# A graph layer's edge loop: VectorE and ScalarE in a written order, node-span products in halves, registers and keys for two chunks at a time

## The chip, the cores and the metric

One core of a Trainium2 chip. The metric is device time in microseconds (us); lower is better. Profile lines are of one profiled execution.

## The reference

12,500 nodes with 32 features, 400,000 edges sorted by their target node, 32 features per edge, a two-layer network on each edge, and a maximum over the edges of a node:

```python
h = jnp.maximum(_layernorm(x, axis=-1), 0.0)
e_feat = jnp.concatenate([h[src], h[dst], edge_attr_32], axis=-1)   # 400000 x 96
hid = jax.nn.relu(e_feat @ W1 + b1)                                 # 96 -> 64
v = hid @ W2 + b2                                                   # 64 -> 32
x_cand = jax.ops.segment_max(v, dst, num_segments=12500)
out = x + jnp.maximum(x_cand, h)
```

## The kernel before

The edges are cut into four stripes, which lie on the four quarters of the partitions. A chunk is 512 edges of each stripe; there are 196 chunks, and the main loop (L363) takes two chunks, a pair, per step. Ahead of it, the kernel computes h, writes it to memory (`h_d`), multiplies it by the target part of W1 (`q_d`) and writes both the keys of the edges whose rows are found by matmul (`key_d`) and the penalties between nodes (`pen_d`). After it, the maxima are merged and added.

One step of the loop does this for its two chunks:

- `gather` (L139): the source rows of h. 12 of a chunk's 16 groups of rows come by indirect DMAs from GpSimd into `gh`, six buffers of one chunk each, 24 DMAs per pair. A buffer is free when VectorE has transposed it (L324).
- `rows_by_matmul` (L278): the other four groups ("tiles") of each chunk, found by TensorE. VectorE makes one-hot matrices out of the keys `kb`: seven `hot` (L285) and one `its` (L287). For a tile, TensorE sums 15 matmuls in a `pv` buffer: one with `its` (L292) and 14 with `hot` (L295). VectorE's maximum (L297) picks the row into `gm`. The generator yields after each tile, and the loop asks for eight tiles per step, for the chunks of the next step.
- `load` (L301): edge features `ea` (SyncE), targets `db` and penalties `pb` (ScalarE's queue), four chunks at once. SyncE loads four registers for a chunk (L314) and fetches four windows of `q_d` by them, `qw` (L318).
- `into_ph` (L375): the first layer, summed in four `ph` buffers out of `ea`, out of `of` and `qw` (`of` is the one-hot matrix of the target, L370), and out of the transposed rows `ht`. `to_features` (L321) makes `ht` by transposes of `gh` (L324) and `gm` (L326).
- ScalarE's relu gives `hid` (L389); the second layer goes into two `pv` buffers (L399); VectorE's scan (L404) gives the running maximum `sm`.
- `leave_1` (L332): TensorE transposes `sm` (L336), VectorE adds b2 (`so`, L338) and makes `last`, which marks the last edge of each node (L340).
- `leave_2` (L346): four matmuls (L350) bring the marked rows to their places in the nodes' windows, ScalarE copies the result to `wo` (L353), and SyncE writes the four blocks on the diagonal to `top_d` by the same registers (L357).

The `pv` pool has three buffers, for tiles and the second layer alike; `tr`, of `leave_1` and `leave_2`, has one. What sets the order:

```python
            tc.manual_schedule(engines={SP, PE}):
```

SyncE and TensorE run as the program is written. On VectorE, ScalarE and GpSimd a scheduler chose the order when the kernel was built. For a pair, VectorE's instructions stand as: two transposes of `gh` for the pair after, two tile maxima, `so`, scan, `its`, scan, maximum, seven `hot`, maximum, a transpose of `gm`, `last`, maximum, `so`, maximum, `last`, `its`, maximum, one `hot`, a transpose of `gm`, six `hot`, two `of`, maximum. On TensorE: `ea`, `of`, tile, `ht`, two tiles, transposes, second layer, two tiles, products (the pair before's second chunk), tile, transposes, tile, products, tile.

Of the kernel before, what the change touches and what calls it, by code (L numbers as in the profile page):

```python
# [18 lines left out]
SP = mybir.EngineType.SP  # L19
PE = mybir.EngineType.PE  # L20
DVE = mybir.EngineType.DVE

P = 128
N = 12500
# [34 lines left out]
def gnn_kernel(ctx, tc, x, src, src_mm, src_t, dst, dst_next, dst_ext, lo, hi, edge_attr, weights, w1, w2, b2, out):  # L59

# [40 lines left out]
    lo_i = const.tile([1, NS, NCH], I32, name="lo_i")  # L101
    nc.sync.dma_start(lo_i, lo.rearrange("(o s) c -> o s c", o=1))

    ident = const.tile([P, P], F32, name="ident")
    make_identity(nc, ident)
# [33 lines left out]
    def gather(c):  # L139
        gh = gathered.tile([P, K, D], F32, name="gh")  # L140
        for k in range(K - MM * (c in MMC)):
            if c * C + k * D < SE:
                nc.gpsimd.indirect_dma_start(  # L143
                    out=gh[:, k, :], out_offset=None, in_=h_d[:, :],
                    in_offset=bass.IndirectOffsetOnAxis(ap=src_i[:, c, k:k + 1], axis=0))
        return gh
# [123 lines left out]

    ea_v = edge_attr.rearrange("s f e -> (s f) e")
    with tc.tile_pool(name="edges", bufs=3) as pool, tc.tile_pool(name="edges_ps", bufs=1, space=PSUM) as ps, \
            tc.manual_schedule(engines={SP, PE}):
        loaded = {}
        windows = {}
        mm_rows = {}

        def rows_by_matmul():  # L278

            for i, c in enumerate(MMC):  # L280
                kb = pool.tile([P, 2, MM * P], F16, name="kb", bufs=2)
                nc.scalar.dma_start(kb, ap(key_d, i * MM * P, [[0, P], [len(MMC) * MM * P, 2], [1, MM * P]]))
                hot = pool.tile([P, A1, MM * P], F32R, name="hot", bufs=2)
                for k in range(A1):
                    nc.vector.tensor_scalar(hot[:, k], kb[:, 0], key_p[:, k:k + 1], None, op0=ALU.is_equal)  # L285
                its = pool.tile([P, MM * P], BF16, name="its", bufs=2)
                nc.vector.tensor_scalar(its, kb[:, 1], place, None, op0=ALU.is_equal)  # L287
                gm = mm_rows[c] = pool.tile([P, MM, D], F32, name="gm", bufs=6)
                for m in range(MM):
                    e = slice(m * P, (m + 1) * P)  # L290
                    po = ps.tile([P, C], F32, name="pv", bufs=3)[:, :D * A0]
                    nc.tensor.matmul(po, its[:, e], others.rearrange("p f a -> p (f a)"), start=True, stop=False)  # L292
                    for k in range(A1):
                        for part in range(2):
                            nc.tensor.matmul(po, hot[:, k, e], hs[:, part, k].rearrange("p f a -> p (f a)"),  # L295
                                             start=False, stop=(k == A1 - 1 and part == 1))
                    nc.vector.tensor_reduce(gm[:, m, :], po.rearrange("p (f a) -> p f a", a=A0),  # L297
                                            axis=AX.X, op=ALU.max)
                    yield

        def load(c):  # L301
            if c % LOAD == 0:
                n = min(LOAD, NCH - c) * C
                ea = pool.tile([P, LOAD * C], F32, name="ea", bufs=2)
                nc.sync.dma_start(ea[:, :n], ea_v[:, c * C:c * C + n])
                db = pool.tile([P, LOAD * C], I32, name="db", bufs=2)
                pb = pool.tile([P, LOAD * C], BF16, name="pb", bufs=2)
                for s in range(NS):
                    g = slice(s * D, (s + 1) * D)
                    nc.scalar.dma_start(db[g, :n], ap(dst_ext, 1 + s * S + c * C, [[0, D], [1, n]]))  # L310
                    nc.scalar.dma_start(pb[g, :n], ap(pen_d, s * S + c * C, [[0, D], [1, n]]))
                for k in range(c, min(c + LOAD, NCH)):
                    loaded[k] = [t[:, (k - c) * C:(k - c + 1) * C] for t in (ea, db, pb)]
            _, base = nc.values_load_multi_w_load_instructions(  # L314
                lo_i[0:1, :, c], engines=[SP], min_val=0, max_val=N)
            qw = pool.tile([P, HID], F32, name="qw", bufs=6)
            for s in range(NS):
                nc.sync.dma_start(qw[s * W:(s + 1) * W, :], q_d[bass.ds(base[s], W), :])  # L318
            windows[c] = qw, base

        def to_features(c, gh):  # L321
            ht = pool.tile([P, K, D], F32, name="ht", bufs=4)
# [6 lines left out]
                nc.vector.memset(ht[:, n:], 0.0)  # L329
            return ht.rearrange("p k e -> p (k e)")  # L330

        def leave_1(c, sm):  # L332
# [6 lines left out]
            last = pool.tile([P, J, NS, W], F32, name="last", bufs=2)  # L339
            nc.vector.tensor_tensor(  # L340
                last, iota_w[:, None, None, :].to_broadcast([P, J, NS, W]),
                at[:, :, c * J:(c + 1) * J].rearrange("p s j -> p j s")[:, :, :, None].to_broadcast([P, J, NS, W]),
                op=ALU.is_equal)
            return so, last

        def leave_2(c, so, last):  # L346

            pw = ps.tile([P, J, P], F32, name="tr")[:, 0]
            for j in range(J):
                nc.tensor.matmul(pw, last[:, j].rearrange("p s w -> p (s w)"), so[:, j, :],  # L350
                                 start=(j == 0), stop=(j == J - 1))
            wo = pool.tile([P, P], F32, name="wo")
            nc.scalar.activation(wo, pw, AF.Copy)  # L353
            _, base = windows.pop(c)
            for s in range(NS):
                g = slice(s * W, (s + 1) * W)
                nc.sync.dma_start(top_d[s % 2][bass.ds(base[s], W), :], wo[g, s * D:(s + 1) * D])  # L357

        tiles = rows_by_matmul()
        for c in range(AHEAD):  # L360
            load(c)
        sm = None
        for c in range(0, NCH, 2):  # L363
            for k in range(c + AHEAD, min(c + AHEAD + 2, NCH)):
                load(k)
            gh = [gather(c + x) for x in range(2)]
            of = []
            for x in range(2):
                of.append(pool.tile([P, C], F32, name="of", bufs=4))
                nc.vector.tensor_scalar(of[x], loaded[c + x][1], node[:, c + x:c + x + 1], None, op0=ALU.is_equal)  # L370


            ph = [ps.tile([P, C], F32, name=f"ph{s}") for s in range(NS)]
# [1 line left out]
            def into_ph(pairs, start, stop):  # L375
                for s in range(NS):
                    g = slice(s * D, (s + 1) * D)
                    for x, (w, e) in enumerate(pairs):
                        nc.tensor.matmul(ph[s][x * HID:(x + 1) * HID], w[g], e[g], start=start, stop=stop)  # L379

            into_ph([(w1c, loaded[c + x][0]) for x in range(2)], True, False)
            into_ph([(windows[c + x][0], of[x]) for x in range(2)], False, False)
            next(tiles, None)
            ht = [to_features(c + x, gh[x]) for x in range(2)]
            into_ph([(w1a, ht[x]) for x in range(2)], False, True)
            hid = []
            for s in range(NS):
                hid.append(pool.tile([P, C], F32, name="hid", bufs=6))
                nc.scalar.activation(hid[s], ph[s], AF.Relu, bias=b1c)  # L389
            next(tiles, None)  # L390
            next(tiles, None)

            if c > 0:
                left = leave_1(c - 1, sm)
            pv = [ps.tile([P, C], F32, name="pv", bufs=3) for x in range(2)]
            for s in range(NS):
                for x in range(2):
# [2 lines left out]
            sms = []  # L400
            for x in range(2):
                before = -LOW if sm is None else sm[:, C - 1:C]
                sm = pool.tile([P, C], F32, name="sm", bufs=4)
                nc.vector.tensor_tensor_scan(sm, loaded.pop(c + x)[2], pv[x], before, op0=ALU.add, op1=ALU.max)  # L404
# [12 lines left out]

    with tc.tile_pool(name="out", bufs=1) as pool:
# [152 lines left out]
```

## Time and profile before

| | |
|---|---|
| median of 3 runs | 5232.83 us (5221.43 to 5245.07) |
| profiled execution | 5227.3 us, span 5225.5 us |
| mean granted clock of TensorE | 0.81 |
| TensorE matmul / weight load busy | 3638.2 us (70%) / 2775.9 us (53%) |
| VectorE busy | 1846.3 us (35%) |
| GpSimd busy | 2238.9 us (43%) |
| ScalarE busy | 315.6 us (6%) |

In the profile, PE is TensorE's matmuls and PEld its weight loads, DVE is VectorE, ACT ScalarE, POOL GpSimd, SP SyncE; a q behind the name means the engine's instruction queue, which issues DMAs and waits. A line of a group reads: line, engine, operation, written tile <- read tiles, shapes, count, then busy us and mean ns of one, then the engine's idle time just before these instructions and what ended it. "issue" is time in which the engine waited for nothing that the profile shows; "remote" is a release that the profile can't put down to an instruction. In the timeline, a line has start and duration in us, and in brackets the idle time before it. Matmul starts are those of the hand-over by TensorE's sequencer, and their ends are modelled. "Records" are single matmuls of the trace: a float32 matmul gives two, all others one.

### The profile page before, as it was taken

Reading aid. Unit: us, or ns where it says so; the run is one execution under the profiler, and the core shown is the slowest. Engines: PE = TensorE matmul, PEld = TensorE weight load, DVE = VectorE, ACT = ScalarE, POOL = GpSimd, SP = SyncE. Lnnn points to the kernel's source line nnn. Section 1 sums busy time; section 2 is a strip of 40 time slices with the busy share of each in tenths; the row PEclk is TensorE's granted clock in tenths of the full one; section 3 lists DMA queues with packets and bytes.
Section 4 is the critical chain, followed back from the end, with each engine's and each line's share of the span. In section 5 each row is a group of like instructions: output and inputs, shape, how many; then the busy total and the mean of one; then the engine's idle time right before and its main releaser. Section 6 shows DMA issues by size and latency. Waiting matters only on the chain. (4 is left out here: it accounts for less than half of the span.)

```text
span 5225.5 us, 57318 instructions
## 1 busy us (share of the span) xinstructions
PE 3638.2 (70%) x20281; PEld 2775.9 (53%) x20281; DVE 1846.3 (35%) x3612; ACT 315.6 (6%) x627; POOL 2238.9 (43%) x2369
## 2 busy tenths in 40 slices
PE   2376767676767676767676767676767676777687
PEld 1255555555555555555554555555555555555565
DVE  2333333333333333333333333333333333333344
ACT  1000000000000000000000000000000000000000
POOL 6534344444444444444444444444444444444420
PEclk6587878787878787878788888787878787878788
DMA  3321112211211121112111211121112211211121
GB/s 123 90 58 43 42 39 58 44 41 40 58 42 41 40 56 44 40 40 56 44 40 40 57 44 40 40 56 44 41 40 57 44 41 40 57 44 40 40 53 65
DMA packets 235577, 256.47 MB, mean 49 GB/s; under 512 B 123653, under 2 KB 211861, under 8 KB 222102
## 3 DMA queue, kind: packets, MB, share of 16 engines
q10 hardware_dynamic: 74084, 137.60, 9.7%
q0 software_dynamic: 75296, 38.70, 5.6%
q1 hardware_dynamic: 85906, 76.48, 4.9%
q8 instruction: 159, 2.61, 0.2%
q14 instruction: 132, 1.08, 0.1%
HBM read 238.44 MB, written 14.04 MB: 48 GB/s over the span
## 5 line engine op out<-in xcount | busy, mean ns | idle before, releaser
L143 POOL DMA_INDIRECT gh<-h_d,src_i x2353 | 2234.8, 950 | 2812.1 <-DVE ht L324 2098.3
L295 PE MATMUL pv<-hs,hot 128*128 128x448 f32 x10808 | 2874.0, 413 | 712.6 <-issue 712.4
L295 PEld LDWEIGHTS pv<-hs,hot 128*128 128x128 f32 x10808 | 2282.8, 212 | 1444.9 <-issue 1270.9
L297 DVE TENSOR_REDUCE gm<-pv 128x32 f32<-128x448 f32 x772 | 481.2, 623 | 2548.3 <-remote 1529.4
L292 PE MATMUL pv<-others,its 128*128 128x448 bf16 x772 | 301.9, 391 | 427.0 <-issue 386.0
L285 DVE TENSOR_SCALAR hot<-kb,key_p 128x512 fp32r<-128x512 f16 x1351 | 555.8, 479 | 9.5 <-DMA qw<-q_d 9.5
L350 PE MATMUL tr<-so,last 128*128 128x128 f32 x1568 | 250.2, 282 | 250.0 <-issue 240.8
L404 DVE TENSOR_TENSOR_SCAN sm<-pb,sm,pv 128x512 f32<-128x512 bf16 x195 | 248.9, 1276 | 469.3 <-remote 332.5
L350 PEld LDWEIGHTS tr<-so,last 128*128 128x128 f32 x1568 | 227.1, 197 | 229.5 <-issue 211.8
L389 ACT ACTIVATE hid<-ph,wt 128x512 f32<-128x512 f32 x392 | 239.3, 690 | 973.5 <-PE ph L379 529.9
L292 PEld LDWEIGHTS <-its 128*128 128x128 bf16 x772 | 78.0, 101 | 400.5 <-issue 387.4
L353 ACT ACTIVATE wo<-tr 128x128 f32<-128x128 f32 x196 | 54.5, 278 | 3810.7 <-remote 1817.6
L336 PE MATMUL tr<-ident,sm 128*128 128x128 f32 x784 | 146.0, 319 | 22.3 <-ACT wo L353 22.3
L336 PEld LDWEIGHTS tr<-ident,sm 128*128 128x128 f32 x784 | 117.9, 167 | 57.9 <-ACT wo L353 38.4
L338 DVE TENSOR_TENSOR so<-tr,wt 128x512 f32<-128x512 f32 x196 | 133.9, 683 | 24.1 <-PE pv L292 11.5
L340 DVE TENSOR_TENSOR last<-iota_w,at 128x512 f32<-128x512 f32 x196 | 131.6, 672 | 28.2 <-PE tr L350 28.2
L324 DVE STREAM_TRANSPOSE ht<-gh 128x384 f32<-128x384 f32 (+1 forms) x196 | 102.9, 563 | 71.0 <-PE ph L379 54.8
L379 PE MATMUL ph<-ea,wt 32*64 32x512 f32 x1568 | 110.0, 617 | 8.4 <-DMA ea<-in_edge_attr 8.4
L379 PE MATMUL ph<-ht,wt 32*64 32x512 f32 x1568 | 110.9, 612 | 0.5 <-issue 0.4
L379 PE MATMUL ph<-of,qw 32*64 32x512 f32 x1568 | 105.5, 592 | 6.2 <-issue 6.2
L399 PE MATMUL pv<-hid,wt 64*32 64x512 f32 x1568 | 108.9, 604 | 0.2 <-ACT hid L389 0.2
L287 DVE TENSOR_SCALAR its<-kb,place 128x512 bf16<-128x512 f16 x193 | 69.6, 361 | 96.4 <-remote 80.1
(68 smaller groups left out, 399.3 us busy)
## 6 DMA issues: line engine op xcount, KB each, us to landing
ea<-in_edge_attr SPq DMA_DIRECT2D x49, 1024.0 KB
db<-in_dst_ext ACTq DMA_DIRECT2D x196, 256.0 KB
kb<-key_d ACTq DMA_DIRECT2D x193, 256.0 KB
gh<-h_d,src_i POOLq DMA_INDIRECT x2353
pb<-pen_d ACTq DMA_DIRECT2D x196, 128.0 KB
qw<-q_d SPq DMA_DIRECT2D x784, 8.0 KB
top_d<-wo SPq DMA_DIRECT2D x784, 4.0 KB
top_d<-zero ACTq DMA_DIRECT2D x2, 1568.0 KB
```

Of the source, the lines that this page charges most:

```text
L143: nc.gpsimd.indirect_dma_start(out=gh[:, k, :], out_offset=None, in_=h_d[:, :], in_offset=bass.IndirectOffsetOnAxis(ap=src_i[:, c, k:k + 1 ...
L285: nc.vector.tensor_scalar(hot[:, k], kb[:, 0], key_p[:, k:k + 1], None, op0=ALU.is_equal)
L292: nc.tensor.matmul(po, its[:, e], others.rearrange("p f a -> p (f a)"), start=True, stop=False)
L295: nc.tensor.matmul(po, hot[:, k, e], hs[:, part, k].rearrange("p f a -> p (f a)"), start=False, stop=(k == A1 - 1 and part == 1))
L297: nc.vector.tensor_reduce(gm[:, m, :], po.rearrange("p (f a) -> p f a", a=A0), axis=AX.X, op=ALU.max)
L336: nc.tensor.transpose(px[:, j, :], sm[:, j * P:(j + 1) * P], ident)
L338: nc.vector.tensor_tensor(so, px, b2r[:, None, :].to_broadcast([P, J, P]), op=ALU.add)
L340: nc.vector.tensor_tensor(last, iota_w[:, None, None, :].to_broadcast([P, J, NS, W]), at[:, :, c * J:(c + 1) * J].rearrange("p s j -> p j ...
L350: nc.tensor.matmul(pw, last[:, j].rearrange("p s w -> p (s w)"), so[:, j, :], start=(j == 0), stop=(j == J - 1))
L379: nc.tensor.matmul(ph[s][x * HID:(x + 1) * HID], w[g], e[g], start=start, stop=stop)
L389: nc.scalar.activation(hid[s], ph[s], AF.Relu, bias=b1c)
L404: nc.vector.tensor_tensor_scan(sm, loaded.pop(c + x)[2], pv[x], before, op0=ALU.add, op1=ALU.max)
```

## The change

- VectorE and ScalarE join the engines whose order is the written one. `rows_by_matmul` is split up: `load_keys`, `one_hots`, `tile_by_matmul`, which returns the maximum as a function that `select` runs later. `of` is made at the end of the step before (`window_hots`), `last` after the second and third tile (`lasts`), the one-hot matrices in two groups, and both chunks of a pair now leave in their own step.
- For a pair, VectorE now runs: transposes of `gh`, `gm`, `gh`, `gm` for this pair, maximum of a0, seven `hot` and `its`, maximum a1, `last`, maximum a2, `last`, two scans, maximum a3, `so`, maximum b0, four `hot`, maximum b1, `so`, three `hot` and `its`, maximum b2, two `of`, maximum b3. TensorE runs: `ea`, `of`, a0, `ht`, a1, a2, second layer, a3, transposes, b0, products, b1, transposes, b2, products, b3. (a and b are the two chunks of the next pair, the figure the tile.) ScalarE issues the eight loads of `db` and `pb` in one row ahead of the relus.
- `leave_2` computes two blocks of 64 nodes' places by 64 columns in place of one of 128 by 128; the other two quarters were never read. `wo` is half as wide.
- SyncE loads the eight registers of two chunks at once from a table laid out for that, and the range tests of their values go.
- One transfer brings the keys of two chunks, half as many transfers of twice the size. `sm` has three buffers in place of four.

```diff
-            tc.manual_schedule(engines={SP, PE}):
+            tc.manual_schedule(engines={SP, PE, DVE, ACT}):
...
+        def load_keys(c):
+            if c in MMC:
+                n = min(2, MMC.stop - c)
+                kb = pool.tile([P, 2, 2, MM * P], F16, name="kb", bufs=2)
+                nc.scalar.dma_start(kb[:, :, :n], ap(key_d, (c - MMC.start) * MM * P,
+                                                     [[0, P], [len(MMC) * MM * P, 2], [1, n * MM * P]]))
+                for k in range(n):
+                    keys[c + k] = kb[:, :, k]
...
+        def one_hots(c, groups):
...
+            for k in groups:
+                nc.vector.tensor_scalar(hot[:, k], keys[c][:, 0], key_p[:, k:k + 1], None, op0=ALU.is_equal)
+            if A1 - 1 in groups:
+                nc.vector.tensor_scalar(its, keys.pop(c)[:, 1], place, None, op0=ALU.is_equal)
...
+            rows = mm_rows[c][:, m, :]
+            return lambda: nc.vector.tensor_reduce(rows, po.rearrange("p (f a) -> p f a", a=A0), axis=AX.X, op=ALU.max)
...
-            _, base = nc.values_load_multi_w_load_instructions(
-                lo_i[0:1, :, c], engines=[SP], min_val=0, max_val=N)
+            if c % 2 == 0:
+                _, base = nc.values_load_multi_w_load_instructions(
+                    lo_i[0:1, c:c + 2], engines=[SP], min_val=0, max_val=N,
+                    skip_runtime_bounds_check_because="dst is a node, or N where the host pads")
...
-            pw = ps.tile([P, J, P], F32, name="tr")[:, 0]
+            pw = ps.tile([P, J, P], F32, name="tr")[:, 0, :2 * D]
             for j in range(J):
-                nc.tensor.matmul(pw, last[:, j].rearrange("p s w -> p (s w)"), so[:, j, :],
-                                 start=(j == 0), stop=(j == J - 1))
-            wo = pool.tile([P, P], F32, name="wo")
+                for g in range(2):
+                    nc.tensor.matmul(pw[g * 2 * W:(g + 1) * 2 * W],
+                                     last[:, j, 2 * g:2 * g + 2].rearrange("p s w -> p (s w)"),
+                                     so[:, j, g * 2 * D:(g + 1) * 2 * D], start=(j == 0), stop=(j == J - 1))
+            wo = pool.tile([P, 2 * D], F32, name="wo")
...
             into_ph([(w1c, loaded[c + x][0]) for x in range(2)], True, False)
-            into_ph([(windows[c + x][0], of[x]) for x in range(2)], False, False)
-            next(tiles, None)
+            into_ph([(windows[c + x][0], ofs.pop(c + x)) for x in range(2)], False, False)
+            tile(a, 0)
             ht = [to_features(c + x, gh[x]) for x in range(2)]
             into_ph([(w1a, ht[x]) for x in range(2)], False, True)
...
-            next(tiles, None)
-            next(tiles, None)
-
-            if c > 0:
-                left = leave_1(c - 1, sm)
+            select()
+            one_hots(b, range(A1))
+            tile(a, 1)
+            select()
+            last = [lasts(c)]
+            tile(a, 2)
+            select()
+            last.append(lasts(c + 1))
             pv = [ps.tile([P, C], F32, name="pv", bufs=3) for x in range(2)]
...
-            next(tiles, None)
-            next(tiles, None)
-            if c > 0:
-                leave_2(c - 1, *left)
-            next(tiles, None)
-            left = leave_1(c, sms[0])
-            next(tiles, None)
-            leave_2(c, *left)
-            next(tiles, None)
-        leave_2(NCH - 1, *leave_1(NCH - 1, sm))
+            tile(a, 3)
+            select()
+            so = leave_1(c, sms[0])
+            tile(b, 0)
+            select()
+            one_hots(a + 2, range(4))
+            leave_2(c, so, last[0])
+            tile(b, 1)
+            select()
+            so = leave_1(c + 1, sms[1])
+            one_hots(a + 2, range(4, A1))
+            tile(b, 2)
+            select()
+            leave_2(c + 1, so, last[1])
+            for k in range(a, min(a + 2, NCH)):
+                window_hots(k)
+            tile(b, 3)
+            select()
```

More of the change, by code (lines that the diff above doesn't have):

```diff
@@ L21 @@
 DVE = mybir.EngineType.DVE
+ACT = mybir.EngineType.Activation
 P = 128
@@ L58, in gnn_kernel @@
 @with_exitstack
-def gnn_kernel(ctx, tc, x, src, src_mm, src_t, dst, dst_next, dst_ext, lo, hi, edge_attr, weights, w1, w2, b2, out):
+def gnn_kernel(ctx, tc, x, src, src_mm, src_t, dst, dst_next, dst_ext, lo, lo_c, hi, edge_attr, weights, w1, w2, b2, out):
     nc = tc.nc
@@ L100, in gnn_kernel @@
     nc.sync.dma_start(src_i.rearrange("p c t -> p (c t)"), src)
-    lo_i = const.tile([1, NS, NCH], I32, name="lo_i")
-    nc.sync.dma_start(lo_i, lo.rearrange("(o s) c -> o s c", o=1))
+    lo_i = const.tile([1, NCH, NS], I32, name="lo_i")
+    nc.sync.dma_start(lo_i, lo_c.rearrange("(o c) s -> o c s", o=1))
     ident = const.tile([P, P], F32, name="ident")
@@ L272, in gnn_kernel @@
     with tc.tile_pool(name="edges", bufs=3) as pool, tc.tile_pool(name="edges_ps", bufs=1, space=PSUM) as ps, \
-            tc.manual_schedule(engines={SP, PE}):
+            tc.manual_schedule(engines={SP, PE, DVE, ACT}):
         loaded = {}
         windows = {}
+        ofs = {}
+        keys = {}
+        hots = {}
+        bases = {}
         mm_rows = {}
[L278 to L299, printed above, removed]
@@ new lines, in load_keys @@
+        def load_keys(c):
[7 more added lines that the diff above has]
+        def one_hots(c, groups):
+            if c not in MMC:
+                return
+            if c not in hots:
+                hots[c] = (pool.tile([P, A1, MM * P], F32R, name="hot", bufs=2),
+                           pool.tile([P, MM * P], BF16, name="its", bufs=2))
+            hot, its = hots[c]
+            for k in groups:
+                nc.vector.tensor_scalar(hot[:, k], keys[c][:, 0], key_p[:, k:k + 1], None, op0=ALU.is_equal)
+            if A1 - 1 in groups:
+                nc.vector.tensor_scalar(its, keys.pop(c)[:, 1], place, None, op0=ALU.is_equal)
@@ new lines, in tile_by_matmul @@
+        def tile_by_matmul(c, m):
+            if c not in MMC:
+                return
+            if m == 0:
+                mm_rows[c] = pool.tile([P, MM, D], F32, name="gm", bufs=6)
+            hot, its = hots[c]
+            e = slice(m * P, (m + 1) * P)
+            po = ps.tile([P, C], F32, name="pv", bufs=3)[:, :D * A0]
+            nc.tensor.matmul(po, its[:, e], others.rearrange("p f a -> p (f a)"), start=True, stop=False)
+            for k in range(A1):
+                for part in range(2):
+                    nc.tensor.matmul(po, hot[:, k, e], hs[:, part, k].rearrange("p f a -> p (f a)"),
+                                     start=False, stop=(k == A1 - 1 and part == 1))
+            rows = mm_rows[c][:, m, :]
+            return lambda: nc.vector.tensor_reduce(rows, po.rearrange("p (f a) -> p f a", a=A0), axis=AX.X, op=ALU.max)
@@ L313, in load, with window_hots @@
                     loaded[k] = [t[:, (k - c) * C:(k - c + 1) * C] for t in (ea, db, pb)]
-            _, base = nc.values_load_multi_w_load_instructions(
-                lo_i[0:1, :, c], engines=[SP], min_val=0, max_val=N)
+            if c % 2 == 0:
+                _, base = nc.values_load_multi_w_load_instructions(
+                    lo_i[0:1, c:c + 2], engines=[SP], min_val=0, max_val=N,
+                    skip_runtime_bounds_check_because="dst is a node, or N where the host pads")
+                for k in range(2):
+                    bases[c + k] = base[k * NS:(k + 1) * NS]
             qw = pool.tile([P, HID], F32, name="qw", bufs=6)
             for s in range(NS):
-                nc.sync.dma_start(qw[s * W:(s + 1) * W, :], q_d[bass.ds(base[s], W), :])
-            windows[c] = qw, base
+                nc.sync.dma_start(qw[s * W:(s + 1) * W, :], q_d[bass.ds(bases[c][s], W), :])
+            windows[c] = qw, bases.pop(c)
+        def window_hots(c):
+            of = ofs[c] = pool.tile([P, C], F32, name="of", bufs=4)
+            nc.vector.tensor_scalar(of, loaded[c][1], node[:, c:c + 1], None, op0=ALU.is_equal)
         def to_features(c, gh):
@@ L330, in to_features, with lasts @@
             return ht.rearrange("p k e -> p (k e)")
+        def lasts(c):
+            last = pool.tile([P, J, NS, W], F32, name="last", bufs=2)
+            nc.vector.tensor_tensor(
+                last, iota_w[:, None, None, :].to_broadcast([P, J, NS, W]),
+                at[:, :, c * J:(c + 1) * J].rearrange("p s j -> p j s")[:, :, :, None].to_broadcast([P, J, NS, W]),
+                op=ALU.is_equal)
+            return last
         def leave_1(c, sm):
@@ L338, in leave_1 @@
             nc.vector.tensor_tensor(so, px, b2r[:, None, :].to_broadcast([P, J, P]), op=ALU.add)
[L339 to L344, printed above, removed]
+            return so
         def leave_2(c, so, last):
-            pw = ps.tile([P, J, P], F32, name="tr")[:, 0]
+            pw = ps.tile([P, J, P], F32, name="tr")[:, 0, :2 * D]
             for j in range(J):
-                nc.tensor.matmul(pw, last[:, j].rearrange("p s w -> p (s w)"), so[:, j, :],
-                                 start=(j == 0), stop=(j == J - 1))
-            wo = pool.tile([P, P], F32, name="wo")
+                for g in range(2):
[3 more added lines that the diff above has]
+            wo = pool.tile([P, 2 * D], F32, name="wo")
             nc.scalar.activation(wo, pw, AF.Copy)
@@ L356, in leave_2 @@
                 g = slice(s * W, (s + 1) * W)
-                nc.sync.dma_start(top_d[s % 2][bass.ds(base[s], W), :], wo[g, s * D:(s + 1) * D])
-        tiles = rows_by_matmul()
+                nc.sync.dma_start(top_d[s % 2][bass.ds(base[s], W), :], wo[g, s % 2 * D:(s % 2 + 1) * D])
+        load_keys(MMC.start)
         for c in range(AHEAD):
             load(c)
+            window_hots(c)
+        one_hots(MMC.start, range(A1))
         sm = None
         for c in range(0, NCH, 2):
+            a, b = c + 2, c + 3
+            gh = [gather(c + x) for x in range(2)]
+            load_keys(a + 2)
             for k in range(c + AHEAD, min(c + AHEAD + 2, NCH)):
                 load(k)
[L366 to L370, printed above, removed]
             ph = [ps.tile([P, C], F32, name=f"ph{s}") for s in range(NS)]
@@ L379, in into_ph, with tile, select @@
                         nc.tensor.matmul(ph[s][x * HID:(x + 1) * HID], w[g], e[g], start=start, stop=stop)
+            waiting = []
+            def tile(c, m):
+                waiting.append(tile_by_matmul(c, m))
+            def select():
+                f = waiting.pop(0)
+                if f:
+                    f()
             into_ph([(w1c, loaded[c + x][0]) for x in range(2)], True, False)
-            into_ph([(windows[c + x][0], of[x]) for x in range(2)], False, False)
-            next(tiles, None)
+            into_ph([(windows[c + x][0], ofs.pop(c + x)) for x in range(2)], False, False)
+            tile(a, 0)
             ht = [to_features(c + x, gh[x]) for x in range(2)]
@@ L402, in gnn_kernel @@
                 before = -LOW if sm is None else sm[:, C - 1:C]
-                sm = pool.tile([P, C], F32, name="sm", bufs=4)
+                sm = pool.tile([P, C], F32, name="sm", bufs=3)
                 nc.vector.tensor_tensor_scan(sm, loaded.pop(c + x)[2], pv[x], before, op0=ALU.add, op1=ALU.max)
                 sms.append(sm)
-            next(tiles, None)
-            next(tiles, None)
-            if c > 0:
-                leave_2(c - 1, *left)
-            next(tiles, None)
-            left = leave_1(c, sms[0])
-            next(tiles, None)
-            leave_2(c, *left)
-            next(tiles, None)
-        leave_2(NCH - 1, *leave_1(NCH - 1, sm))
+            tile(a, 3)
[16 more added lines that the diff above has]
+            select()
     with tc.tile_pool(name="out", bufs=1) as pool:
@@ L553 @@
         "lo": np.ascontiguousarray(dp[:, ::C]),
+        "lo_c": np.ascontiguousarray(dp[:, ::C].T),
         "hi": np.ascontiguousarray(dp[:, np.minimum(np.arange(C, S + 1, C), SE) - 1]),
```

## The prediction

> **What bounds the kernel now.** I read the page first, then fifty-microsecond windows over the run, then the timeline of one loop step, then the order of the instructions on each engine.
>
> ```profile
> L143 POOL DMA_INDIRECT gh<-h_d,src_i x2353 | 2234.8, 950 | 2812.1 <-DVE ht L324 2098.3
> L295 PE MATMUL pv<-hs,hot 128*128 128x448 f32 x10808 | 2874.0, 413 | 712.6 <-issue 712.4
> L297 DVE TENSOR_REDUCE gm<-pv 128x32 f32<-128x448 f32 x772 | 481.2, 623 | 2548.3 <-remote 1529.4
> L350 PE MATMUL tr<-so,last 128*128 128x128 f32 x1568 | 250.2, 282 | 250.0 <-issue 240.8
> ```
>
> No engine is full: PE 70%, GpSimd 43%, VectorE 35%. GpSimd waits 2098.3 us for VectorE's transposes. VectorE waits 1529.4 us for something unnamed before the reductions. PE stands 712.4 us on "issue". The windows (time, then PE, weight loads, VectorE, ScalarE, GpSimd, clock, DMA share, GB/s) say when:
>
> ```profile
> 2500.00:2550.00 50.00, 37.88 (x213) 28.94 (x213) 18.16 (x36) 2.98 (x6) 21.77 (x23) 0.84 0.10 20
> ...
> 5100.00:5150.00 50.00, 50.00 (x335) 40.41 (x328) 30.86 (x62) 5.40 (x10) 0.00 (x0) 1.00 0.14 36
> ```
>
> With gathers running, PE gets 213 matmuls into 50 us. Near the end, gathers gone and nothing else changed, it gets 335. A pair of chunks needs about 207 matmul records: 31 us without gathers, and 51.6 us with them (first gathers of the pairs from 280.11 to 5030.77, 92 steps). The timeline of one step shows the loss:
>
> ```profile
> 2521.50 0.95 POOL L143 DMA_INDIRECT gh<-h_d,src_i  x1 [23.02 <-DVE ht L324]
> ...
> 2528.07 3.13 PE L295 MATMUL pv<-hs,hot 128*128 128x448 f32 x14
> ...
> 2531.50 1.28 DVE L404 TENSOR_TENSOR_SCAN sm<-pb,sm,pv 128x512 f32<-128x512 bf16 x1 [3.60 <-PE pv L295]
> ...
> 2546.23 0.53 PE L295 MATMUL pv<-hs,hot 128*128 128x448 f32 x1 [1.57 <-issue]
> ...
> 2550.28 0.95 POOL L143 DMA_INDIRECT gh<-h_d,src_i  x1 [0.30 <-issue]
> ...
> 2553.24 0.62 DVE L297 TENSOR_REDUCE gm<-pv 128x32 f32<-128x448 f32 x1 [18.08 <-remote]
> ...
> 2555.33 2.40 PE L295 MATMUL pv<-hs,hot 128*128 128x448 f32 x6 [0.87 <-issue]
> ```
>
> The pair's 24 gathers run from 2521.50 to 2551.23. The tile handed out at 2528.07 should be done at 2531.2; its reduction starts at 2553.24. Before that, PE hands out one instruction each 0.7 to 2.1 us. So PE's completions are held back while gathers run, and 2 to 4 us longer. By program order, the reduction at 2553.24 closes the 120th PE instruction (load or matmul) since the first gather: a rest of 20, tile 30, transposes 8, the second-layer matmuls 32, tile 30. The first 58 come at full speed, the 32 take until 2531.5 to 2533.6, the last 30 take 20 us (0.7 us each). PE has by then handed out some 64 more (a tile of 15, 8 products, about 9 of the next tile, each with its load), and goes no further ahead. At 2555.33 the hold ends, 33.8 us after the first gather; the rest to the next first gather (2572.54) is 17.2 us of unbroken PE work. This is the limit: a hold of 33.8 us tied to the gathers, plus what PE still has to do after it.
>
> **The change part by part.** (a) *Registers.* Each chunk had a load of 0.87 us and four range tests, about 1.9 us on SyncE. A pair saves one load and eight tests, near 3 us. PE's wait for the windows that SyncE fetches is 6.2 us in the whole run (L379, of and qw), so 0 us, at most 6.
>
> (b) *Keys.* 193 transfers become 97. An issue takes 0.38 us of ScalarE, 6% busy: 0 us. Without that cover it would be 96 x 0.38 = 36 us of gain.
>
> (c) *ScalarE's order.* In every second pair, the eight broadcast loads and the keys now stand in one row before the four relus. Loads 1.6 us apart (2569.83, 2571.53, 2573.39, 2574.70) put the relus some 9 us after the first gather, finished at 11. The second-layer matmuls behind them could go at 11 at full speed, and wait until about 12 anyway (e). I take 0; without the cover 1 to 2 us in every second pair.
>
> (d) *Halves.* Each of the four products per chunk becomes two of 64 rows and 64 columns. PE instructions per chunk go from 16 to 32. Now eight matmuls take 0.9 us, one each 0.11 us (row of 2510.10: 8 loads in 1.06 us). No row has this form. Below, half the columns and both halves beside each other give 0.45 us; the sixteen matmuls of L379, on separate parts of the array, take 1.11 us together though each takes 0.6. Above, 16 x 0.11 = 1.8 us. I take 0.9, no change, since each is half as wide and they are twice as many.
>
> The Trainium skill (TensorE: Matmul & The Clock Gate, LDWEIGHTS) puts a weight load at columns over 1.2 GHz; 64 columns would be 53 ns and sixteen 0.85 us, an estimate that would leave the sum unchanged.
>
> (e) *VectorE's order: the part that decides.* Before, the scheduler put the transposes of gathered rows (L324) a pair ahead, after this pair's ht matmuls (2519.34). They start the gathers. Now they stand behind the reduction of the previous pair's last tile and before this pair's ht matmuls. The gathers thus start when PE has just finished ea and of. By the step above: a last tile handed out at 2511.18 has its reduction at 2514.38; with 0.62 + 0.58 + 0.25 us the first gather starts near 2515.8 instead of 2521.5. What PE runs freely now covers tile a0 and the ht matmuls, 72 instructions that used to lie before the gathers.
>
> Counted from the first gather, completions now are: a0 30, ht 62, a1 92, a2 122, second layer 154. By the row of before (90 at 10 to 12 us, 120 at 29 to 34 us), a1 is reduced near 12 and a2 near 29 to 34. PE may hand out 64 more, but tile a3 needs the pv buffer of a2 (three buffers in turn, and the second layer takes the two others). So PE stands at a3 until a2 is reduced. The scans, which before ran inside the hold, come after it too.
>
> What is left at the end of the hold, at rates of before: a3 about 5.0 (0.37 us a matmul, clock 0.50), transposes 0.7, b0 to b3 4 x 3.05 = 12.2, products 2 x 0.9 = 1.8, transposes 0.65, then reduction, transpose and start 1.5. That is 21.9 us against 17.2. The same sum for before gives 17.1: rest of a tile 2.2, transposes 0.8, three tiles 9.1, products 0.95, ea and of 2.0, ht 1.2, transposes 0.9. VectorE in that stretch has some 12 us of work in 22, so it adds nothing. Each step loses 4.7 us; 93 steps lose 437 us. The profiled execution took 5227.3 us (span 5225.5), 5.5 under the median, so 5664, taken as 5660.
>
> On the clock: in windows of 4 us from 2544 to 2552 the granted clock is 0.50 with PE at 1.07 us busy, and at 1.00 from 2508 to 2540. The skill's page on the clock gate (The HAM clock gate) says that an idle window of about 3.4 us halves the clock. Standing before a3 would bring more such windows; by that rule a3 runs wholly at half rate (5.6 us), by the row the estimate above.
>
> Unknown sizes: the products 0.45 to 1.8 us each move a step by -0.9 to +1.8 us (-84 to +167 us). A reduction of a2 at 29 or at 34 us moves it by -2.5 to +0.7 us.
>
> **Rivals.** *1. The hold passes work, not instructions.* If the same PE work gets through, the ht matmuls (32 instructions, 1.2 us) cost little, a2 is reduced early and a3 runs within the hold. The step stays within 0.6 us: 5230 to 5285 us. For it: both readings fit the first 5.6 us. Against: the 32 second-layer instructions, 1.1 us of work, used 3.3 us and more of the hold.
>
> *2. Faster: SyncE's instructions fill the same path.* If what holds PE is shared among all engines, every range test removed near the first gather frees 0.72 us (the 30-instruction tile over its 20 us). The second chunk's load and eight tests (2519.14 to 2521.0) are nine: 6.5 us, less 4.7, is 1.8 us gained per step: 5060 us. It decides from seven instructions on. Against: they lie before the first gather, when nothing is held.
>
> *3. The change as written.* The order of the built kernel shows the transposes before the reduction of a0, and the first gather of a pair waiting for the first of them. That part does happen; there is no case in which it doesn't.
>
> **How the numbers follow.** My forecast 0.75 (own range 5480 to 5880: the sum with the unknowns, and a hold a little longer or shorter); rival 1 0.12, half within 0.5% and half just above; rival 2 0.13. Half a percent (26 us) is about what a measurement of this kernel tells from no change. Faster 0.13, same 0.06, slower 0.81. The range runs from 5250, which leaves out rival 2 and most of "same", to 5880.
>
> **What would show it.** Right: the first gather of a pair starts between the of matmuls and tile a0; steps of 55 to 57 us; after the scans, four tiles and more lie between the hold and the next gather; the reduction of a2 is the one with the long wait. Wrong: steps of 52 us or less, the scans well before the last gather, or PE at a steady rate through the gathers. In the last case the hold isn't tied to the gathers, and the forecast falls with it.

## The result, and the profile after

The changed kernel takes 5605.26 us (median of 4 runs, 5594.57 to 5621.0) and the kernel before, beside it, 5227.13 (4 runs, 5197.55 to 5245.07): ratio 1.073, interval 1.067 to 1.079. The profiled execution took 5610.15 us, span 5608.4, mean granted clock 0.775. The forecast was 5660, slower.

Costliest groups of the page of the changed kernel (line, engine, operation, tiles, count, then busy us and mean ns, then idle time before and its releaser):

```profile
L144 POOL DMA_INDIRECT gh<-h_d,src_i x2353 | 2283.4, 970 | 3200.6 <-DVE ht L355 2436.9
L317 PE MATMUL pv<-hs,hot 128*128 128x448 f32 x10808 | 2718.9, 398 | 280.5 <-issue 277.7
L320 DVE TENSOR_REDUCE gm<-pv 128x32 f32<-128x448 f32 x772 | 481.7, 624 | 3580.2 <-remote 2398.3
L446 PE MATMUL pv<-hid,wt 64*32 64x512 f32 x1568 | 352.9, 1026 | 1396.4 <-DVE gm L320 1116.3
L383 PE MATMUL tr<-so,last 128*64 128x64 f32 x3136 | 134.9, 229 | 3.8 <-DVE so L375 3.8
```

VectorE's idle time before its maxima grew from 2548.3 to 3580.2 us. TensorE's "issue" time before the tiles' matmuls fell from 712.4 to 277.7 us, and the second layer now waits 1116.3 us for a maximum. The products have become twice as many and cost 134.9 us busy in place of 250.2. One step, from the end of a hold to the end of the next (timeline: start, duration, then what ran):

```profile
2521.12 0.62 DVE L320 TENSOR_REDUCE gm<-pv 128x32 f32<-128x448 f32 x1 [25.92 <-remote]
...
2521.80 1.95 PE L446 MATMUL pv<-hid,wt 64*32 64x512 f32 x14 [15.79 <-DVE gm L320]
...
2523.74 3.66 PE L317 MATMUL pv<-hs,hot 128*128 128x448 f32 x14
...
2530.83 0.55 PEld L383 LDWEIGHTS tr<-so,last 128*64 128x64 f32 x16 [0.30 <-issue]
2530.83 0.69 PE L383 MATMUL tr<-so,last 128*64 128x64 f32 x16
...
2542.67 1.06 PE L413 MATMUL ph<-of,qw 32*64 32x512 f32 x16
...
2543.25 0.94 POOL L144 DMA_INDIRECT gh<-h_d,src_i  x1 [25.69 <-DVE ht L355]
...
2543.67 0.36 PE L314 MATMUL pv<-others,its 128*128 128x448 bf16 x1
...
2551.75 0.62 DVE L320 TENSOR_REDUCE gm<-pv 128x32 f32<-128x448 f32 x1 [7.92 <-PE pv L317]
...
2577.08 0.62 DVE L320 TENSOR_REDUCE gm<-pv 128x32 f32<-128x448 f32 x1 [21.65 <-remote]
```

The first gather starts between the `of` matmuls and tile a0, as the forecast had it. The maximum of a0 follows 8.5 us later, that of a1 33.8 us later, after the last of the 24 gathers. Then come the second layer, five tiles, two sets of transposes and two of products, `ea` and `of`, all unbroken, until the next first gather at 2600.18.

Over the steps with 24 gathers (92 in the trace before, 94 after) I measured from the first gather to the tile maximum that ends VectorE's longest gap between two maxima, and from there to the next first gather. The medians are 33.80 and 18.93 us before, 33.86 and 23.09 after. The hold has not changed. In the median it ends 4.1 us behind the last gather before and 3.6 behind it after, so its length is that of the row of 24 gathers, issued 1.25 us apart, and some 4 us more. What TensorE does behind it grew by 4.2 us, and 92 steps of that are 383 us; the medians of the runs differ by 378.

### The profile page after: what moved, and what is told of

The parts are those of the page before. It is cut to its first block, busy times and chain, and to the rows that moved or that the text cites. A ratio compares the mean times of both kernels' runs of the same rounds, so it can differ in the third digit from the quotient of the medians.

```text
span 5608.4 us, 58542 instructions
## 1 busy us (share of the span) xinstructions
PE 3566.3 (64%) x21849; PEld 2536.3 (45%) x21849; DVE 1831.2 (33%) x3612; ACT 323.2 (6%) x627; POOL 2287.5 (41%) x2369
## 5 line engine op out<-in xcount | busy, mean ns | idle before, releaser
L144 POOL DMA_INDIRECT gh<-h_d,src_i x2353 | 2283.4, 970 | 3200.6 <-DVE ht L355 2436.9
L317 PE MATMUL pv<-hs,hot 128*128 128x448 f32 x10808 | 2718.9, 398 | 280.5 <-issue 277.7
L317 PEld LDWEIGHTS pv<-hs,hot 128*128 128x128 f32 x10808 | 2169.5, 202 | 724.1 <-issue 569.4
L320 DVE TENSOR_REDUCE gm<-pv 128x32 f32<-128x448 f32 x772 | 481.7, 624 | 3580.2 <-remote 2398.3
L446 PE MATMUL pv<-hid,wt 64*32 64x512 f32 x1568 | 352.9, 1026 | 1396.4 <-DVE gm L320 1116.3
L446 PEld LDWEIGHTS pv<-hid,wt 64*32 64x32 f32 x1568 | 42.2, 134 | 1603.9 <-DVE gm L320 1226.8
L387 ACT ACTIVATE wo<-tr 128x64 f32<-128x64 f32 x196 | 43.9, 224 | 3276.8 <-PE tr L383 3273.7
L383 PE MATMUL tr<-so,last 128*64 128x64 f32 x3136 | 134.9, 229 | 3.8 <-DVE so L375 3.8
L383 PEld LDWEIGHTS tr<-so,last 128*64 128x64 f32 x3136 | 107.7, 138 | 62.7 <-issue 57.8
L373 PE MATMUL tr<-ident,sm 128*128 128x128 f32 x784 | 119.2, 275 | 13.3 <-DVE sm L451 12.6
L373 PEld LDWEIGHTS tr<-ident,sm 128*128 128x128 f32 x784 | 99.0, 143 | 31.1 <-DVE sm L451 14.5
```

The costliest lines, as they stand in the source:

```text
L144: nc.gpsimd.indirect_dma_start(out=gh[:, k, :], out_offset=None, in_=h_d[:, :], in_offset=bass.IndirectOffsetOnAxis(ap=src_i[:, c, k:k + 1 ...
L320: return lambda: nc.vector.tensor_reduce(rows, po.rearrange("p (f a) -> p f a", a=A0), axis=AX.X, op=ALU.max)
L383: nc.tensor.matmul(pw[g * 2 * W:(g + 1) * 2 * W], last[:, j, 2 * g:2 * g + 2].rearrange("p s w -> p (s w)"), so[:, j, g * 2 * D:(g + 1) * ...
L446: nc.tensor.matmul(pv[x][s * D:(s + 1) * D], w2x[g], hid[s][g], start=True, stop=True)
```

## Experiments

They ran in three sets, on three chips. On that of the first set the kernel before takes 3193.56 us (3191.09 to 3194.03), on that of the third 3192.65 (3190.68 to 3196.01), and neither shows a hold; the second set ran where it takes 5235.63 (5215.65 to 5255.44). I tell the second set first, since it answers the prediction's questions. A "step" is the distance between the first copies to `wo` of two neighbouring pairs, averaged; steps without and with ScalarE's eight loads are told apart.

### Where the kernel before takes 5235.63 us

**The changed kernel again.**

> The changed kernel as it is. Of the two variants run so far beside the kernel before at 3193.56 us, one step of two chunks took 31.2 us where ScalarE loads nothing and 36.4 where it issues its row of eight loads. Theory of the row (ScalarE issues eight loads ahead of the relus, each waits for an earlier transfer, and PE stands for hid): if the kernel before takes about 3190 us here, the changed one takes 3340 to 3400, with steps of about 31 and 36 us in turn. If the kernel before takes about 5230 here, the steps are of one length, about 56 us, and it takes 5590 to 5640. Rival (the order by itself makes every step longer): steps of one length in both cases.

5595.2 us (5589.76 to 5612.15), ratio 1.068 (1.064 to 1.071). Steps 56.6 us without the row of loads and 56.0 with it: one length, within 0.6 us. Both the theory of the row and its rival expected this of this chip.

**Loads behind the relus.** In `load`, the eight transfers are only noted, and issued after the relus:

```diff
+                late.append((c, n, db, pb))
...
                 nc.scalar.activation(hid[s], ph[s], AF.Relu, bias=b1c)
+            load_late()      # four db, then four pb
```

> The changed kernel with one edit: ScalarE's eight loads are issued behind the four relus of their step, four db and then four pb, not ahead of them. Theory of the row: if the kernel before takes about 3190 us, the steps with loads fall from 36.4 to about 31 us, 49 steps x 5.2 us = 255 us, and it takes 3100 to 3190, no slower than the kernel before. If the kernel before takes about 5230, it changes nothing, 5560 to 5640, since the first gather and not the row sets the step there. Rival (the order of VectorE's work or the stand at tile a3 is what costs): it stays within 1 per cent of the changed kernel.

5602.83 us, steps 56.1 without loads and 56.2 with: no change. Where there is a hold, part (c) costs nothing, as the forecast took it.

**The gathers' place.** To the kernel above, one edit: VectorE's transposes of gathered rows, which free the buffers and start the gathers, stand behind the maximum of a0 and are for the pair after.

```diff
+            gh = [gather(k) for k in (a, b) if k < NCH]
+            ht = [to_features(c + x) for x in range(2)]   # gm rows only
...
             select()                                      # maximum of a0
+            for k, g in zip((a, b), gh):
+                gathered_rows(k, g)
```

> The changed kernel with two edits: the eight loads behind the relus, and the transposes of the gathered rows a pair ahead, behind the maximum of tile a0, so that the next pair's gathers start late in a step. If the kernel before takes about 3190: the second edit alone cost or gave under 1 per cent, so 3090 to 3200, at the loads-after-relus kernel plus or minus 30 us. If about 5230: theory of the place of the gathers (they start in PE's work and a hold follows) 5080 to 5300; rival (the hold takes the same 33 us of PE's instructions wherever it lies) 5550 to 5650.

5071.29 us (5054.59 to 5083.11), ratio to the kernel before 0.969 (0.965 to 0.972), 9 us under the theory's range. Against the kernel with the loads alone that is 531.5 us less, 5.8 per step. The forecast had derived that the change starts the gathers 5.7 us earlier in TensorE's work; put back by about that much, the time comes back. The timeline of one step of this kernel:

```profile
2465.36 1.11 PE L429 MATMUL ph<-ht,wt 32*64 32x512 f32 x16
...
2466.85 0.94 POOL L144 DMA_INDIRECT gh<-h_d,src_i  x1 [20.37 <-DVE ht L362]
...
2481.24 0.62 DVE L322 TENSOR_REDUCE gm<-pv 128x32 f32<-128x448 f32 x1 [4.43 <-PE pv L319]
...
2500.20 0.62 DVE L322 TENSOR_REDUCE gm<-pv 128x32 f32<-128x448 f32 x1 [16.14 <-remote]
...
2517.81 0.94 POOL L144 DMA_INDIRECT gh<-h_d,src_i  x1 [20.61 <-DVE ht L362]
```

The gathers now start behind the `ht` matmuls. a1, a2, the second layer and a3 are done 14.4 us later (2481.24), with both scans; the maximum of b0 ends the hold at 2500.20, 33.35 us after the first gather, and 17.6 us of work are left. (Over all steps the measure of hold and rest gives medians of 28.8 and 21.8 us here, since in some steps another gap of VectorE is the longest; the mean step is 50.6.) This is also the fastest version measured on this chip, 164 us below the kernel before; which part of the order gives those 164 us was not separated.

**Registers and halves alone.** The kernel before, with the scheduler's order, and `values_load` per two chunks and `leave_2` as in the change.

> The kernel before with two parts of the change alone: registers per two chunks without the bounds check, and the node spans in halves; the order of VectorE and ScalarE stays the scheduler's. Registers cost nothing either way; the halves take 16 products in 0.69 us in the place of 8 in 1.05, 0.36 us per chunk, 196 x 0.36 = 71 us at most where PE sets the step. If the kernel before takes about 3190: 3110 to 3200. If about 5230: 5130 to 5260. Rival (the halves lengthen PE's work, as 8 more instructions per chunk, or the scheduler orders otherwise because of them): 3200 to 3300, or 5260 to 5400.

5292.3 us (5285.1 to 5300.64), ratio 1.011 (1.008 to 1.014): 57 us slower, above the range for such a chip and in the rival's (the halves lengthen PE's work, or the order changes with them). VectorE's order in the loop is that of the kernel before in this trace, and ScalarE's differs only in where the `db` loads stand among the relus, so a new order hardly explains it. The medians by step are a hold of 33.10 and a rest of 20.05 us, against 33.80 and 18.93. Which of the two parts did it was asked by the registers alone, but that run came on a chip without the hold (below).

### Where the kernel before takes about 3193 us

**No gathers.** In both kernels `gather` returns one fixed buffer, so that only its first chunk of rows is ever fetched.

> The kernel before, in which only the rows of the first chunk are gathered and stand in for those of all chunks (the other gathers are left out). Theory: without gathers completions aren't held back; PE sets the step at 31.2 us, 98 steps are 3060 us, with about 200 us ahead and 30 behind: 3290 (3200 to 3400). If the hold had another cause, the run would stay above 4500.

> The changed kernel, with the same gathers left out. Theory: the new order costs nothing by itself, PE sets the step; with the halves 30.5 us: 3220 (3130 to 3330), not above the kernel before without gathers by more than 1%. Rival (the written order makes PE wait for VectorE or ScalarE whatever the gathers do): 5 to 8% above it.

3176.2 us for before, under the range, and 3312.9 for after, a single time each. On this chip all the gathers of the kernel before are worth 17 us, so there is no hold to remove; TensorE's busy share of the span is 96% without them. Yet the changed order is 4.3% slower, more than the theory's 1% and a little less than the rival's 5 to 8%: here the written order does make TensorE wait. Steps before: 31.1 us without loads and 31.2 with; after, 30.7 and 34.6, so the loss lies in the steps with loads.

**The whole product** (`leave_2` as before, 128 x 128), and **the rows a pair ahead** with the loads still in their row:

> The changed kernel with the whole 128 by 128 product of before. Theory (place of the gathers in the step decides): the changed kernel's product takes 0.69 us for 16 matmuls, before's took 1.05 for 8; both products of a step lie after the hold, so a step grows by 0.7 us and the run by 92 x 0.7 = 66 us, to about 5670 (5630 to 5710). Rival (the 32 further PE instructions of the halves cost time where completions are held back): the run falls by 0.7 us for each of the 32 in the hold, 23 us a step at most; anything below 5560 would speak for it.

> The changed kernel with one thing put back: the transposes of the gathered rows stand a pair ahead, behind the maximum of tile a0, so that the gathers start after this pair's ht matmuls. Theory: the rest after the hold falls back from 19.6 to 16.2 us or less (the halves save 0.7 us more); step 51.5 us, run about 5160 (5080 to 5260). Rival (ScalarE's row of loads, the keys or the halves make the loss): the run stays near 5600 (5500 to 5650).

3427.73 us (ratio 1.073, 1.072 to 1.075) and 3393.71 (1.062, 1.059 to 1.064). Neither expectation can be judged on a chip without the hold. But the steps showed where this chip loses: 31.2 without loads and 36.4 with them in the one, 30.7 and 36.3 in the other. ScalarE's timeline of a step with loads, kernel with the whole product:

```profile
1571.34 0.38 ACTq L288 DMA_DIRECT2D kb<-key_d  x1
1571.76 0.48 ACTq L331 DMA_DIRECT2D db<-in_dst_ext  x1
1572.28 0.43 ACTq L332 DMA_DIRECT2D pb<-pen_d  x1
1577.22 0.32 ACTq L331 DMA_DIRECT2D db<-in_dst_ext  x1
...
1581.21 0.31 ACTq L332 DMA_DIRECT2D pb<-pen_d  x1
1587.76 0.32 ACTq L331 DMA_DIRECT2D db<-in_dst_ext  x1
1588.12 0.43 ACTq L332 DMA_DIRECT2D pb<-pen_d  x1
1588.60 2.42 ACT L431 ACTIVATE hid<-ph,wt 128x512 f32<-128x512 f32 x4 [17.06 <-DMA qw<-q_d]
```

Seven of the nine issues are shown. They take 0.3 to 0.5 us each, and up to 6.2 us lie between two of them, in which ScalarE's queue waits for earlier transfers by the profile's semaphores (4.5 us ahead of 1577.22, 6.2 ahead of 1587.76). The `ht` matmuls had been done at 1580.3. Then, on TensorE and VectorE:

```profile
1589.34 3.65 PE L444 MATMUL pv<-hid,wt 64*32 64x512 f32 x16 [2.88 <-ACT hid L431]
...
1593.02 2.66 DVE L449 TENSOR_TENSOR_SCAN sm<-pb,sm,pv 128x512 f32<-128x512 bf16 x2 [5.30 <-PE pv L444]
```

The second layer stands for `hid`, then follows the relus one by one in 3.65 us where it needs 1.09, partly at clock 0.50 (for 3.41 us from 1590.14). In the kernel before (here without gathers) the scheduler had put one load ahead of the first relu, three between them, and `pb` behind:

```profile
1524.18 0.34 ACTq L315 DMA_DIRECT2D db<-in_dst_ext  x1
1525.87 0.69 ACT L394 ACTIVATE hid<-ph,wt 128x512 f32<-128x512 f32 x1 [8.77 <-PE ph L384]
...
1536.35 1.73 ACTq L316 DMA_DIRECT2D pb<-pen_d  x4
```

**Four and two bursts of gathers.** Loads behind the relus and rows a pair ahead, with the transposes of half a chunk behind four maxima, or of a chunk behind two.

> The kernel with the loads behind the relus and the transposes a pair ahead (5071.29 us beside a kernel before at 5235.63), with one edit: a pair's 24 gathers are split into four lots of six, each behind its own transpose, and the transposes stand behind four different maxima of the step, so that the gathers come in four bursts of some 7.6 us and not in one of 30. In one burst PE runs freely for its first 10 to 13 us and is held back for the other 20. Theory A (each burst gives PE its free first microseconds anew): little is held back, a step falls from 50.5 us to 33 to 42, 3400 to 4200 us. Theory B (the hold is a rate: PE loses a fixed time per gather, 20 us by 24 gathers): 4950 to 5200. On a chip where the kernel before takes about 3190: 3090 to 3200, no tale about the hold.

> The same with two bursts of twelve gathers, one per chunk, some 15 us each, in two places of the step. Theory A (the free time is had anew in each burst): two times some 3 to 5 us are held back and not one time 20, a step of 38 to 46 us, 3800 to 4650 us, between one burst and four. Theory B (a fixed loss per gather): 4950 to 5200. On a chip where the kernel before takes about 3190: 3090 to 3200.

**The whole product, with the loads behind the relus and the rows a pair ahead.**

> The kernel with the loads behind the relus and the transposes a pair ahead (5071.29 us beside 5235.63 for the kernel before), with the node spans as one product of 128 x 128 again. It prices the halves under the order by hand. Theory from the kernel with registers and halves (plus 57 us against the kernel before): the halves put 32 more PE instructions into a step, which costs some 0.6 us where instructions are held back, so without them 4990 to 5060. Rival (they save 0.36 us per chunk, as in the trace of the changed kernel): 5090 to 5150. On a chip where the kernel before takes about 3190: 3150 to 3260, 71 us above the same kernel with halves.

3152.09 us (ratio 0.987, 0.986 to 0.989), 3178.75 (0.996, 0.994 to 0.997) and 3177.13 (0.995, 0.993 to 0.997). All three are faster than the kernel before (3192.65 here), by 0.4 to 1.3%, and within the ranges given for such a chip; their question about the hold stays open, because there was none. What they show is the row of loads: with it behind the relus, the steps with loads take 31.2, 31.9 and 31.2 us, where they had taken 36.4 and 36.3. The list of waits says it too. First the kernel with the whole product and the loads ahead, then the one with the whole product, the loads behind and the rows a pair ahead (total us, count, longest):

```profile
PEld pv L444 <- ACT hid L431: 208.4, 194, 5.0
...
PE pv L444 <- ACT hid L431: 129.0, 48, 4.6
```

```profile
PEld pv L463 <- ACT hid L447: 3.0, 4, 1.7
PE pv L463 <- ACT hid L447: 0.8, 1, 0.8
```

These three kernels differ from the two before them in the gathers' place or the product as well as in the loads, so no pair isolates the row here; that only the steps with loads changed, and the waits for `hid` went, is what puts it down to the row. Two bursts are slower than four in the steps with loads alone (31.9 against 31.2). VectorE waits 246.0 us in all for gathers that have not landed, against 122.5 with four bursts; that this is the cause is not shown.

The halves on these chips, from the steps without loads: 31.2 with the whole product, 30.7 with halves. The products' busy time, whole (first) and in halves (the kernel with four bursts):

```profile
L395 PE MATMUL tr<-so,last 128*128 128x128 f32 x1568 | 206.6, 275 | 3.8 <-DVE so L388 3.8
```

```profile
L401 PE MATMUL tr<-so,last 128*64 128x64 f32 x3136 | 134.8, 228 | 4.0 <-DVE so L393 4.0
```

Half a microsecond per step, 0.25 per chunk, some 48 us in all: a gain.

**Registers alone.**

> The kernel before with SyncE's registers read per two chunks and unchecked, nothing else. With the halves beside them it was 1.07 per cent slower (5292.3 against 5235.63 us). If the registers cost nothing, as forecast, this is within 0.5 per cent of the kernel before, and the 57 us are the halves'. Rival (SyncE now issues its fetches in a burst at another place of the step, and that is what cost): 5265 to 5310. On a chip where the kernel before takes about 3190: within 0.5 per cent.

3191.97 us, ratio 0.9995 (0.9986 to 1.0005): nothing, as forecast. So the 57 us of registers and halves on the chip with the hold are probably the halves', which add 32 instructions to a step; this wasn't shown there.

This kernel differs from the one before in the registers alone, and its page shows what a chip without the hold does with the gathers in place:

```profile
PE 3055.8 (96%) x20281; PEld 2467.5 (77%) x20281; DVE 1854.2 (58%) x3612; ACT 316.2 (10%) x627; POOL 2347.5 (74%) x2369
```

GpSimd issues the gathers 1.25 us apart, as on the chip with the hold. They fill 30 of a step's 31.2 us, and TensorE is busy for 96% of the span beside them. So gathers in flight don't hold TensorE back by themselves; no run shows what has to be added.

## Why the prediction was right

**The limit.** Right: a hold tied to the gathers, 33.8 us from the first gather, plus the work behind it. The hold is the same after, moving the gathers alone moved 531.5 us, and in the trace before, the three steps behind the last gather take 31.2 us each. That its 33.8 is also the median of 33.80 is chance: the forecast's hold ends where TensorE runs unbroken again, and up to the maximum (2553.24) its step has 31.7. Its step of 51.6 us should be 52.2, since 91 steps lie between the two first gathers that it names, not 92. Wrong in its inner rule: about 120 instructions per hold was no constant. From the first gather to the end of the tile whose maximum ends the hold, the traces have a median of 117 before, 92 in the changed kernel (a0, `ht`, a1) and 153 in the one with the rows ahead (a1, a2, second layer, a3, transposes, b0). Nor is it a fixed amount of work, as rival 1 had it: at full-speed durations these are about 7 and 14 us.

**(a) and (b), registers and keys: 0.** Registers are shown to be nothing, on the chip without the hold. Keys were not tried alone.

**(c) ScalarE's row: 0, under its cover.** The cover is the hold, behind which the relus' delay disappears. Right where it exists: 5602.83 against 5595.2 us. The second layer is held till 2577.76 anyway. The price without the cover was the mis-sized one: I wrote 1 to 2 us in every second pair, from loads 1.6 us apart, and on the chips without the hold it is 5.2 (36.4 less 31.2). The loads don't follow each other at a fixed distance; each can wait for an older transfer.

**(d) Halves: 0.9 us per chunk, no change.** Sixteen products take 0.69 us of the trace, against about 1.05 for eight whole ones. The sixteen weight loads, for which the forecast had an estimate of 0.85 us, took 0.55. Yet the run of registers and halves was 57 us slower under the hold. There the first set of products lies in the held part, where one instruction takes some 0.7 us; that this costs more than their work saves is argued and not shown.

**(e) The order: 4.7 us per step, 437 in all.** Right in mechanism; 4.2 was measured for the whole change. What the halves do to it under this order was not measured with the hold. I multiplied by 93 steps, and by the first gathers there are 91 between those two moments, 92 with the end: at 92, 4.7 gives 432. The rest of 21.9 us was nearly right by errors that cancel. In the step shown, from 2521.12 to 2543.25, it is 22.1 us; the median is 23.09. It holds 2.6 us of second layer that I had put inside the hold, because a1 and not a2 ends the hold (the one sign that I named and that came out wrong): of the three `pv` buffers the second layer takes those of a0 and a1, so TensorE stands in the second layer for a1's maximum and not at a3 for a2's. a3 took 3.4 us to the transposes in this step and 4.2 in the median, not 5.0, and the products 0.6 twice, not 0.9.

**The clock.** The granted clock (last column but two) around the end of a hold:

```profile
2552.17:2555.58 3.41, 1.01 (x3) 0.74 (x4) 3.26 (x9) 0.26 (x1) 2.80 (x3) 1.00 0.09 14
...
2555.00:2577.00 22.00, 8.48 (x14) 3.10 (x13) 0.43 (x2) 2.75 (x4) 14.23 (x15) 0.51 0.08 12
2577.00:2581.00 4.00, 3.24 (x18) 1.46 (x19) 3.54 (x5) 0.00 (x0) 0.00 (x0) 0.50 0.02 4
2581.00:2585.00 4.00, 4.00 (x18) 3.63 (x18) 2.01 (x4) 0.00 (x0) 0.00 (x0) 0.76 0.00 0
2585.00:2600.00 15.00, 15.00 (x119) 12.41 (x125) 8.08 (x18) 0.45 (x2) 0.00 (x0) 1.00 0.18 43
```

The clock is full for the first 12 us of this hold, half from 2555.58, and full again from 2582.89, 5.1 us after the second layer went on. The Trainium skill (TensorE: Matmul & The Clock Gate, Part 1: The HAM clock gate) says that an idle window of about 3.4 us halves the clock and a busy one of as much restores it. The lengths agree: the half stretch is 27.31 us, eight times 3.41, and the last 3.41 us ahead of 2582.89 are the first wholly busy ones. But the 3.41 us ahead of 2555.58 were not idle; they held 1.01 us of matmuls. What the forecast missed is which work pays first: the second layer takes the beginning of the slow stretch, and a3 what is left of it. That varies: in the step shown further up the clock was full 1.2 us into a3, and over the 92 holds of the trace a3 ran at the full clock for 28% of its time in the median.

**The rivals.** 1: not seen; the step grew by 4.2 us, not 0.6 at most. 2: not seen; with fewer instructions on SyncE the changed kernel and the one with registers and halves were slower under the hold, and the registers alone brought nothing without it. 3: the change does what is written.

**What the number owes to the chip.** The slowdown of the changed kernel itself was measured with the hold only. On a chip without it, its two nearest relatives lose 6 to 7% as well, but to another part of the change, the one that I had priced at nothing. The same sign there would not have made the argument right.

## What to carry to other kernels

When one stretch of a step has a fixed length, count what has to run behind it, and start it as late in the other engines' work as the data allow: moving two transposes behind the next tile and the `ht` matmuls was worth 531.5 us of 5602.83. When an engine's order is written by hand, keep the DMA issues of a compute engine behind the operations that others wait for; each issue can wait for an older transfer, and a row of nine delayed four relus by 8 us. Price an edit with its cover and without: the cover may be missing elsewhere, and then the edit that cost nothing is what decides.

## What the runs showed of the hardware that I had not expected

One chip of this kind holds TensorE's completions back while GpSimd's gathers run and two others don't: the same kernel takes 5235.63, 3193.56 and 3192.65 us. Its step is 52.2 us with the hold (in the trace before) and about 31.2 without it (in the run with registers alone), and the gathers, at the same pace, cost 17 us where there is no hold. What differs between the chips was not settled, nor what sets how many instructions a hold lets through. Whether smaller bursts of gathers shorten the hold was asked, and not answered.
